# Attention scores of a decoder layer as float32r products over 64 rows of high and low parts, spread by transfers with 32 rows as outer dimension, and the maxima kept on the chip

## The chip, the cores and the metric

The kernel runs on one core of one Trainium2 chip. The metric is the device time of one execution in microseconds (us), as a median of several runs. PE is the engine for matrix products (PEld its weight loads), DVE, ACT and POOL work on vectors, and SP only issues transfers (DMA) here, all on one queue, in order. An engine works through its instructions in the order in which they were written to it.

## What is computed

For each of 32 batches of 256 tokens with 256 channels, the reference computes one decoder layer. All arrays are float32.

```
x = layernorm(x + ssm(x))                    # state-space mixer, 512 inner channels, 16 states
x = layernorm(x + attention(x, ctx, ctx))    # 16 heads of 16 channels, 256 keys
x = layernorm(x + experts(x))                # 8 experts, each with 32 tokens of every batch, 704 wide

scores = einsum('bhqd,bhkd->bhqk', q, k) / sqrt(16)
attn   = softmax(scores)                     # over the 256 keys
```

The mixer has a recurrence over the tokens, in chunks of 64, for each of 512 x 16 states. The change concerns the scores: `q` and `k` are 16 channels per head, and the softmax subtracts each query's largest score before the exponential.

## The kernel before, in words

**Stages.** The program holds no loop with waits of its own choice: a planner, run while the program is written, holds a clock for each engine, a cost for each kind of instruction (`MM`, `EV`, `VE`, `CV`, `GP`, L307 to L311) and some twenty chains of work (L1255 to L1276). `in_order` (L80) lets the chain whose next step can start first take its step, and so fixes the order of instructions on each engine for good. Semaphores then make each instruction wait for its data. The chains are the mixer (`pres`, `steps`, `decays`, `scan`, `weighted`, `sums`), the attention (`keys_ahead`, `keys`, `mixes`, `queries`, `maxima`, `attns`, `finishes`), the experts (`units`, `fetches` and others, in two sets of buffers), and `rest` (L364), which issues the transfers of weights that are needed later.

**The mixer.** Each batch takes 16 steps of 32 inner channels. A step loads `ld` by two transfers of 256 KB (L519), ACT makes the decays `da` (L573, four instructions), DVE makes the product `bu` (L602) and the recurrence `h` (L621), POOL multiplies `h` by `c_bc` (L637), and after every four steps PE sums the states into `y` (L651). There are 512 steps. There are six buffers for `h`, and three steps of `ld` are loaded ahead. Between these instructions the planner puts those of the other chains.

**The attention of a batch.**
- Keys are made some batches ahead (L691): PE `ps_qk`, ACT adds the bias into `k_flat` (two halves of 128 channels, L706), and a transfer stores it to `k_all` in DRAM (L710). The values take the same buffer afterwards. Queries do the same with `q_flat` and a DRAM tile `heads` (L801 to L806).
- `spread_heads` (L678) loads them back from DRAM so that a head's 16 channels lie at rows 0 to 15 (even heads) or 64 to 79 (odd heads) of `kT` and `qT`, eight heads (one half of the 16) with two transfers of 64 KB. The other rows of `qT` are zero; row 63 of each half of `kT` is one, all through the run (L271 to L277).
- `maxima` (L825) takes two heads at a time: `scores` (L809) issues four products of 63 rows (two heads on the two halves of PE's rows, two halves of the queries) into two PSUM banks; DVE takes the maximum over the keys (L838) into `tops`. After eight heads PE transposes `tops` (L844), ACT negates it into `rows` (L847), a transfer stores `rows` to DRAM (L852), and another loads them into row 63 of `qT` (L855).
- `attns` (L874) makes the scores again, keys against queries, over 64 rows: since row 63 of `kT` is one and that of `qT` the negated maximum, they come out lowered. ACT takes the exponential from PSUM (L894), PE multiplies by the values (L863), and `finish` (L924) divides, projects, normalizes and stores the batch to `x2d` (L969).

**The experts.** A unit is two blocks of 128 rows of four batches each (L978). For batches 24 to 31 a unit holds two experts for one group of four batches, so its last four units need batch 31 from `x2d`. A unit has products `ps_h` (L1133) and `ps_down` (L1212), and units are what the planner puts between the other work on PE. At most five PSUM banks (`RING`) serve everything but `bu` and `b_bc`.

The functions that the change touches, and their callers:

## Time and profile before

| | |
|---|---|
| runs | 2744.45, 2734.66, 2743.19 us; median 2743.19 |
| profiled execution | 2743.78 us, of which the span from the first to the last instruction is 2742.0 |
| busy, share of the span | PE 2466.3 us (90%), DVE 2380.6 (87%), ACT 2043.4 (75%), POOL 1643.7 (60%) |
| transfers | 505.86 MB in 491497 packets; the queue of SP fills 64.8% of 16 engines' span |
| mean granted PE clock | 0.959 |
| SP's waits on the maxima | 67.8 us for `rows` (ACT), 45.1 us for the store of `tops` |

How to read the rows. A line of groups has the source line, the engine, the operation, `output<-input`, the shapes and the count, then the busy time in us and the mean of one in ns, then the engine's idle time just before them and what ended most of it. A line of waits says who waited for whom: us in total, how often, the longest. The chain of work that ended last goes back from the last instruction, at each step to what released it; its rows are start and length in us. One product of float32 shows as two records of PE, and busy time counts overlapping records once. A row of stages has its bounds, its length, and the busy time and number of instructions of each engine.

The middle of the run is alike from some 140 us to 2500 us: the recurrence goes on, and the attention and experts of earlier batches run beside it. After the last recurrence the attention of the last batch is left, with the expert units that still wait, and after that batch's store four units.

### The profile page before, as it was taken

Reading aid. Unit: us, or ns where it says so; the run is one execution under the profiler, and the core shown is the slowest. Engines: PE = TensorE matmul, PEld = TensorE weight load, DVE = VectorE, ACT = ScalarE, POOL = GpSimd, SP = SyncE. Lnnn points to the kernel's source line nnn. Section 1 sums busy time; section 2 is a strip of 40 time slices with the busy share of each in tenths; the row PEclk is TensorE's granted clock in tenths of the full one; section 3 lists DMA queues with packets and bytes.
Section 4 is the critical chain, followed back from the end, with each engine's and each line's share of the span. In section 5 each row is a group of like instructions: output and inputs, shape, how many; then the busy total and the mean of one; then the engine's idle time right before and its main releaser. Section 6 shows DMA issues by size and latency. Waiting matters only on the chain.

```text
span 2742.0 us, 48659 instructions
## 1 busy us (share of the span) xinstructions
PE 2466.3 (90%) x16964; PEld 1705.3 (62%) x16964; DVE 2380.6 (87%) x2413; ACT 2043.4 (75%) x4327; POOL 1643.7 (60%) x1145
## 2 busy tenths in 40 slices
PE   5788989889899899989998989999999899998988
PEld 4565666566566666666666666665666566666767
DVE  4999999999999999999999999999999899896212
ACT  6887888888778878887878778888788788674331
POOL 4775766666666666575666665666666666553000
PEclk8899999999999999998999999999999999999999
DMA  7866666666676666676666666667666566666464
GB/s 203 228 199 176 193 187 181 189 191 191 187 199 186 181 167 190 176 197 177 167 198 187 198 175 186 187 177 195 190 197 179 163 172 180 185 174 181 150 195 144
DMA packets 491497, 505.86 MB, mean 184 GB/s; under 512 B 177204, under 2 KB 339252, under 8 KB 491252
## 3 DMA queue, kind: packets, MB, share of 16 engines
q1 hardware_dynamic: 491252, 502.75, 64.8%
q8 instruction: 135, 2.21, 0.4%
q14 instruction: 110, 0.90, 0.1%
HBM read 426.07 MB, written 76.55 MB: 183 GB/s over the span
## 4 chain that ended last, share of the span: by engine, by line
PE 29%; DVE 11%; ACT 8%; DMA 5%; issue 3%; POOL 1%; SPq 1%; DVEq 0%; ACTq 0%; POOLq 0%
PE ps_h L1133 8%; PE s L816 6%; DVE h L621 5%; PE ps_down L1212 4%; ACT da L573 3%; PE y L651 3%; DVE bu L602 2%; DVE tops L838 2%; PE ps_in L349 2%; PE ps_oT L863 2%; DMA ld<-dd 1%; DMA xe<-x2d 1%; PE ps_out L349 1%; PE ps_qk L349 1%; ACT es L894 1%
## 5 line engine op out<-in xcount | busy, mean ns | idle before, releaser
L637 POOL TENSOR_TENSOR h<-h,c_bc 128x1024 f32<-128x1024 f32 x512 | 1209.1, 2362 | 740.6 <-DVE h L621 627.0
L621 DVE TENSOR_TENSOR_SCAN h<-da,bu 128x1024 f32<-128x1024 f32 x512 | 1168.9, 2283 | 50.4 <-ACT da L573 5.8
L573 ACT ACTIVATE da<-ld,a_neg 128x252 f32<-128x252 f32 x2048 | 864.6, 504 | 188.3 <-DVE h L621 138.4
L602 DVE TENSOR_TENSOR bu<-ld,b_bc 128x1024 f32<-128x1024 f32 x512 | 626.1, 1223 | 19.9 <-DMA ld<-dd 8.0
L816 PE MATMUL s<-kT,qT 63*128 63x256 f32 x2048 | 345.4, 416 | 45.6 <-DVE tops L838 22.8
L894 ACT ACTIVATE es<-s 128x512 f32<-128x512 f32 x512 | 277.9, 594 | 140.6 <-PE s L816 75.9
L838 DVE TENSOR_REDUCE tops<-s 128x2 f32<-128x512 f32 x512 | 325.2, 677 | 41.6 <-PE s L816 41.1
L1133 PE MATMUL ps_h<-x2T,w 128*128 128x256 f32 (+2 forms) x1536 | 343.5, 368 | 9.5 <-ACT es L894 1.7
L816 PE MATMUL s<-qT,kT 64*128 64x256 f32 x2048 | 313.8, 405 | 22.5 <-DMA qT<-tops 13.0
L651 PE MATMUL y<-h,sel_y 128*32 128x256 f32 x4096 | 280.8, 397 | 52.3 <-POOL h L637 36.9
L816 PEld LDWEIGHTS s<-kT,qT 63*128 63x128 f32 x2048 | 213.8, 193 | 151.9 <-DVE tops L838 50.8
L1133 PEld LDWEIGHTS ps_h<-x2T,w 128*128 128x128 f32 (+1 forms) x1536 | 246.7, 186 | 89.7 <-issue 35.1
L349 PE MATMUL ps_in<-xT,w_in 128*128 128x256 f32 x1024 | 258.4, 397 | 8.7 <-ACT da L573 2.6
L816 PEld LDWEIGHTS s<-qT,kT 64*128 64x128 f32 x2048 | 200.9, 189 | 102.3 <-issue 39.6
L651 PEld LDWEIGHTS y<-h,sel_y 128*32 128x32 f32 x4096 | 131.8, 113 | 177.4 <-POOL h L637 55.1
L349 PEld LDWEIGHTS ps_in<-xT,w_in 128*128 128x128 f32 x1024 | 192.8, 196 | 60.4 <-issue 12.9
L420 POOL TENSOR_TENSOR u<-u,shifted 128x512 f32<-128x512 f32 x128 | 151.4, 1183 | 39.7 <-ACT u L407 34.7
L323 POOL TENSOR_SCALAR ln_rstd<-ln_mv 128x2 f32<-128x2 f32 x96 | 20.9, 218 | 254.2 <-DVE ln_mv L320 250.0
L407 ACT ACTIVATE shifted<-ps_in,tap_b,conv_w 128x256 f32<-128x256 f32 x256 | 130.8, 567 | 22.5 <-PE ps_in L349 10.9
L863 PE MATMUL ps_oT<-es,v 128*32 128x256 f32 x2048 | 142.4, 391 | 3.7 <-DVE h L1197 1.2
L349 PE MATMUL ps_out<-w_out,yg 128*128 128x256 f32 x512 | 117.6, 383 | 0.4 <-DVE yg L667 0.4
L375 ACT ACT_TABLE_LOAD x90 | 115.5, 1283 | 1.4
(135 smaller groups left out, 2987.5 us busy)
## 6 DMA issues: line engine op xcount, KB each, us to landing
ld<-dd SPq DMA_DIRECT2D x1024, 256.0 KB
w<-in_w SPq DMA_DIRECT2D x128, 352.0 KB
x<-in_x SPq DMA_DIRECT2D x64, 256.0 KB
dd<-delta SPq DMA_DIRECT2D x32, 512.0 KB
dd<-u SPq DMA_DIRECT2D x32, 512.0 KB
w<-in_w SPq DMA_DIRECT2D x32, 384.0 KB
w13y<-in_w SPq DMA_DIRECT2D x32, 352.0 KB
c_bc<-bcd SPq DMA_DIRECT2D x64, 128.0 KB
```

What stands on the lines that cost most here:

```text
L349: nc.tensor.matmul(ps[:, j, :], l, r, start=(k == 0), stop=(k == len(terms) - 1))
L420: nc.gpsimd.tensor_tensor(u[:, cc], u[:, cc], at, ALU.add)
L573: nc.scalar.activation(da[:, g, q].rearrange("p (k t) -> p k t", t=CHUNK)[:, :, 1:], loads[i][:, 0, g].rearrange("p (k t) -> p k t", t=CHU ...
L602: nc.vector.tensor_tensor(bu, loads[i][:, 1].unsqueeze(2).to_broadcast([P, GB, NQ, L]), b_bc.unsqueeze(1).to_broadcast([P, GB, NQ, L]), AL ...
L621: nc.vector.tensor_tensor_scan(h.rearrange("p g q t -> p (g q t)"), das_of.pop(i).rearrange("p g q t -> p (g q t)"), bu.rearrange("p g q t ...
L637: nc.gpsimd.tensor_tensor(hs[i], hs[i], c_bc, ALU.mult)
L651: nc.tensor.matmul(y[32 * j : 32 * j + 32, :], sel_y[:, g, :], hs[i - NJ + 1 + j][:, g, q, :], start=(g == 0 and q == 0), stop=(g == GB - ...
L816: nc.tensor.matmul(s[:, t, :], left[r : r + n, g, t * P : (t + 1) * P], right[r : r + n, g, :], start=True, stop=True,)
L838: nc.vector.tensor_reduce(top[:, h % 2, h // 2, :], s, AX.X, ALU.max)
L863: nc.tensor.matmul(oT[32 * j : 32 * j + 32, :], v[:, k, 4 * g + j, :], ess[j][:, k, :], start=(k == 0), stop=(k == 1), tile_position=(0, 3 ...
L894: nc.scalar.activation(es, s, AF.Exp, scale=1.0 / DK**0.5)
L1133: nc.tensor.matmul(ps[:m, i, :], w_tiles[u, which, e][k][:, f * P : f * P + m], right, start=(k == 0), stop=(k == 1),)
```

## The change

The scores are made from two parts of each number. POOL copies `k_flat` (`q_flat`) to a float32r tile `hi`, which rounds it, and takes `lo` = full - `hi` in place (new `parts_of`). Both parts go to DRAM, and they come back so that each head has 64 rows, which hold, for each of the 16 channels, the four combinations of a part of `q` with a part of `k`. So one float32r product over 64 rows gives the score. To get these rows, the query's transfer reads 32 rows (part, channel) and writes each twice, 256 KB a transfer with runs of 4 KB; the key's transfers read 32 rows (channel, part) and write them once each, 128 KB, two for the two copies. Weights' columns and the biases are reordered so that the channel is the outer index; POOL does it for `w_k` and `w_q` at the start (`ordered`), and all but one of the late transfers go out before it.

The maxima don't go to DRAM. POOL copies `tops` to `padded` in high and low parts, PE transposes it twice (128 rows each), and ACT writes the negated maxima as `mT`. In `attns` a second product adds them to the scores in PSUM: weights `pick`, which has ones at the two rows (high and low) of the head, on all 128 columns, times `mT`. So `maxima` has the same number of products as before, and `attns` twice as many. Row 63 of `kT` and `qT` and their fills are gone. The planner's costs are changed in places (`MM`, `EV`, `VE`, `CV`, `GP`, and those of layer norm, decays and scan), which moves instructions of all chains.

The diff, cut to what the text speaks of:

```diff
@@ -115,7 +116,7 @@
 
     x2d = dram.tile([B, L, D], F32, name="x2d")
 
-    k_all = dram.tile([B, D, L], F32, name="k_all")
+    k_all = dram.tile([B, DK, 2, 2 * NG, 2, L], F32, name="k_all")
     v_all = dram.tile([B, L, D], F32, name="v_all")
 
     ph = ctx
@@ -163,18 +164,31 @@
         dma(t, a[name].partition_broadcast(P))
         return t
 
-    def heads(n):
+    def heads(n, tag):
 
         w = wp.tile([P, 2, D], F32, tag="w_" + n, name="w_" + n)
+        raw = unit1.tile([P, 2, D], F32, tag=tag, name="raw_" + n)
         src = a["w_" + n].rearrange("(k p) (h c) -> p k h c", p=P, c=32)
         for k in range(2):
-            dst = w[:, k].rearrange("p (h c) -> p h c", c=DK)
+            dst = raw[:, k].rearrange("p (h c) -> p h c", c=DK)
             dma(dst, src[:, k, :, :DK])
         bias = wp.tile([P, 2], F32, name="b_" + n)
-        for g in range(NG):
-            r = 64 * (g % 2)
-            src = a["b_" + n].rearrange("(j c) g -> j c g", c=32)[:, :DK, g : g + 1]
-            dma(bias[r : r + 64, g // 2 : g // 2 + 1], src)
+        src = a["b_" + n].rearrange("(g1 j c) (i g2) -> j g2 g1 c i", g1=2, j=2, c=32, g2=2)
+        for j in range(2):
+            for g in range(NG):
+                dma(bias[NG * j + g :: 2 * NG, :], src[j, g // 2, g % 2, :DK])
+
+        def ordered():
+            for k in range(2):
+                for i in range(2):
+                    at = slice(i * P, (i + 1) * P)
+                    nc.gpsimd.tensor_copy(
+                        w[:, k, at].rearrange("p (c j g) -> p g j c", j=2, c=DK),
+                        raw[:, k, at].rearrange("p (g j c) -> p g j c", j=2, c=DK),
+                    )
+            spend("POOL", 1.6)
+
+        orders.append(ordered)
         return w, bias
 
 
@@ -206,13 +220,13 @@
             dma(at, src[j, g].unsqueeze(1).to_broadcast([DL, NL, NDC * NS]))
     nc.scalar.preload_act_table_set("natural_log_exp_and_others")
 
-    later = []
+    later, orders = [], []
     now, dma = dma, lambda dst, src: later.append((dst, src))
-    w_k, b_k = heads("k")
+    w_k, b_k = heads("k", "att")
     w_v = weight("w_v", D, D)
     b_out = row("b_out")
     w_out = weight("w_out", DI, D)
-    w_q, b_q = heads("q")
+    w_q, b_q = heads("q", "oT")
     w_o = weight("w_o", D, D)
     b_o = row("b_o")
     b_v = wp.tile([P, 2, 1], F32, name="b_v")
@@ -268,13 +282,22 @@
     nc.gpsimd.memset(v[:, :, :, DK : DK + 1], 1.0)
 
 
-    kT = keep.tile([P, HG, L], F32, name="kT")
-    last = small.tile([P, 1], F32, tag="ln_st", name="last")
-    at = ident.rearrange("p (j c) -> p j c", c=HR)[:, :, HR - 1]
-    nc.vector.tensor_reduce(last, at, AX.X, ALU.add)
-    nc.vector.tensor_copy(kT.rearrange("p g t -> p (g t)"), last.to_broadcast([P, HG * L]))
-    qT = keep.tile([P, HG, L], F32, name="qT")
-    nc.gpsimd.memset(qT, 0.0)
+    kT = keep.tile([P, HG, L], F32R, name="kT")
+    qT = keep.tile([P, HG, L], F32R, name="qT")
+    mTs = [keep.tile([P, L], F32R, name=f"mT_{i}") for i in range(2)]
+    padded = keep.tile([P, 2, 2, HR], F32R, name="padded")
+    nc.gpsimd.memset(padded.bitcast(F32), 0.0)
+    pick = keep.tile([P, HG], F32R, name="pick")
+    picked = small.tile([P, HG], F32, tag="ln_st", name="picked")
+    nc.vector.tensor_reduce(
+        picked.rearrange("p (i g) -> p i g", i=2),
+        ident.rearrange("p (j r) -> p j r", r=HR)[:, :, : 4 * NG].rearrange(
+            "p j (i s g) -> p i g j s", i=2, s=2
+        ),
+        AX.XY,
+        ALU.add,
+    )
+    nc.vector.tensor_copy(pick, picked)
 
     tops = [keep.tile([P, 2, 4, 2], F32, name=f"tops_{i}") for i in range(2)]
 
@@ -304,11 +327,11 @@
         return ps_mm.tile([P, 2 * L], F32, tag="mm", name=name)
 
 
-    MM = 0.47
-    EV = {1: 0.47, 2: 0.6, 4: 1.06}
-    VE = {1: 0.41, 2: 0.69, 4: 1.23}
-    CV = 0.565
-    GP = {1: 0.7, 2: 1.27, 4: 2.36}
+    MM = 0.49
+    EV = {1: 0.42, 2: 0.56, 4: 1.05}
+    VE = {1: 0.41, 2: 0.66, 4: 1.225}
+    CV = 0.535
+    GP = {1: 0.7, 2: 1.23, 4: 2.36}
 
     def layernorm(tiles, t):
 
@@ -330,7 +353,7 @@
             nc.scalar.activation(
                 x, x, AF.Identity, bias=off[:, i, :], scale=rstd[:, i, :]
             )
-        return spend("ACT", 0.6 * n)
+        return spend("ACT", 0.55 * n)
 
     def transposes(src):
 
@@ -363,9 +386,13 @@
 
     def rest():
 
-        while later:
+        while len(later) > 1:
             yield 0.0, "SP"
             dma(*later.pop(0))
+        yield clock.at["SP"] + 2 * LANDING, "POOL"
+        while orders:
+            orders.pop(0)()
+        dma(*later.pop(0))
 
     xps, dds, sress, bcds, ygs, us, spread, silus = {}, {}, {}, {}, {}, {}, {}, []
     gated, stored = {}, []
@@ -576,7 +603,7 @@
                         AF.Exp,
                         scale=a_neg[:, j, g, c * NQ + q : c * NQ + q + 1],
                     )
-            decayed[i] = spend("ACT", GB * NQ * 0.5)
+            decayed[i] = spend("ACT", GB * NQ * 0.43)
 
     read = {-1: 0.0}
 
@@ -626,7 +653,7 @@
                 op0=ALU.mult,
                 op1=ALU.add,
             )
-            recurred[i] = spend("DVE", 2.29)
+            recurred[i] = spend("DVE", 2.285)
             read[i] = max(multiplied, decayed[i])
 
     def weighted():
@@ -675,6 +702,23 @@
     kts, qts, tts, vts, x1Ts, attended, oSs, ending = {}, {}, {}, {}, {}, [], [], []
     scored = {}
 
+    def parts_of(n, b, full, t, d):
+
+        hi = unit1.tile([P, 2, L], F32R, tag="hi", name=f"{n}_hi_{b}")
+        lo = full.bitcast(F32R)
+        yield t, "POOL"
+        nc.gpsimd.tensor_copy(hi, full)
+        nc.gpsimd.tensor_tensor(lo, full, hi.bitcast(F32), ALU.subtract)
+        t = spend("POOL", 2 * GP[2])
+        yield t, "SP"
+        for s, part in enumerate((hi, lo)):
+            part = part.bitcast(F32)
+            if n == "q":
+                dma(d[:, s].rearrange("i c x t -> (c x) i t"), part)
+            else:
+                at = d[:, s].rearrange("c x i t -> c x (i t)")
+                dma(at, part.rearrange("p i t -> p (i t)"))
+
     def spread_heads(b, dst, d, t, there):
 
         yield t, "SP"
@@ -682,8 +726,16 @@
             if b:
                 yield lambda: max(t, scored[b - 1, half]) if (b - 1, half) in scored else None, "SP"
             for j in range(2):
-                src = d.rearrange("(i g j c) t -> i j c g t", i=2, j=2, c=DK)[half, j]
-                dma(dst[HR * j : HR * j + DK, 4 * half : 4 * half + 4, :], src)
+                at = dst[HR * j : HR * (j + 1), NG * half : NG * (half + 1), :].bitcast(F32)
+                if dst is qT:
+                    src = d[half, :, :, NG * j : NG * (j + 1)]
+                    src = src.rearrange("s c g t -> (s c) (g t)").unsqueeze(1)
+                    at = at.rearrange("p g t -> p (g t)")
+                    dma(at, src.to_broadcast([2 * DK, 2, NG * L]))
+                else:
+                    src = d[:, :, NG * j : NG * (j + 1), half].rearrange("c s g t -> (c s) g t")
+                    for s in range(2):
+                        dma(at[2 * DK * s : 2 * DK * (s + 1)], src)
             there[b, half] = clock.at["SP"] + LANDING
 
     made = []
@@ -706,8 +758,7 @@
             flat = unit1.tile([P, 2, L], F32, tag="k_flat", name=f"k_flat_{b}")
             tk = biased(flat, AF.Identity, b_k, ps, 0)
             done(1, tk)
-            yield tk, "SP"
-            dma(k_all[b].rearrange("(m p) t -> p m t", p=P), flat)
+            yield from parts_of("k", b, flat, tk, k_all[b])
             yield from take(1, rank, t0)
             ps, t = product(
                 "ps_v",
@@ -801,13 +852,11 @@
             flat = unit1.tile([P, 2, L], F32, tag="q_flat", name=f"q_flat_{b}")
             tq = biased(flat, AF.Identity, b_q, ps, 0)
             done(1, tq)
-            yield tq, "SP"
-            d = bcd.tile([D, L], F32, tag="heads", name="heads")
-            dma(d.rearrange("(m p) t -> p m t", p=P), flat)
+            d = bcd.tile([2, 2, DK, 2 * NG, L], F32, tag="heads", name="heads")
+            yield from parts_of("q", b, flat, tq, d)
             yield from spread_heads(b, qT, d, clock.at["SP"] + LANDING, qts)
 
-    def scores(heads, left, right, n):
-
+    def scores(heads, left, right, lowered):
 
         ss = [bank("s").rearrange("p (t n) -> p t n", t=2) for _ in heads]
         for t in range(2):
@@ -815,12 +864,22 @@
                 g, r = h // 2, HR * (h % 2)
                 nc.tensor.matmul(
                     s[:, t, :],
-                    left[r : r + n, g, t * P : (t + 1) * P],
-                    right[r : r + n, g, :],
+                    left[r : r + HR, g, t * P : (t + 1) * P],
+                    right[r : r + HR, g, :],
                     start=True,
-                    stop=True,
+                    stop=not lowered,
                 )
-        return ss, spend("PE", 2 * MM + 0.2)
+            for h, s in zip(heads, ss):
+                g, r = h // 2, HR * (h % 2)
+                if lowered:
+                    nc.tensor.matmul(
+                        s[:, t, :],
+                        pick[r : r + HR, g : g + 1].to_broadcast([HR, P]),
+                        mTs[g // NG][r : r + HR, :],
+                        start=False,
+                        stop=True,
+                    )
+        return ss, spend("PE", 0.7 if lowered else 0.4)
 
     def maxima():
 
@@ -832,28 +891,30 @@
             h = 0
             while h < 8:
                 yield from take(2, 2, t0)
-                ss, ts = scores(range(8 * half + h, 8 * half + h + 2), qT, kT, HR - 1)
+                ss, ts = scores(range(8 * half + h, 8 * half + h + 2), qT, kT, False)
                 for s in ss:
                     yield ts, "DVE"
                     nc.vector.tensor_reduce(top[:, h % 2, h // 2, :], s, AX.X, ALU.max)
                     t = spend("DVE", VE[2])
                     done(1, t)
                     h += 1
+            yield t, "POOL"
+            r = 2 * NG * half
+            hi, lo = padded[:, :, :, r : r + NG], padded[:, :, :, r + NG : r + 2 * NG]
+            full = top.rearrange("p j g t -> p t j g")
+            nc.gpsimd.tensor_copy(hi, full)
+            nc.gpsimd.tensor_tensor(lo, full, hi.bitcast(F32), ALU.subtract)
+            t = spend("POOL", 0.5)
             yield from take(1, 1, t)
-            ps = bank("ps_m")[:H, :P]
-            nc.tensor.transpose(ps, top.rearrange("p j g t -> p (j g t)"), ident)
-            yield spend("PE", 0.2), "ACT"
-            rows = unit2.tile([H, P], F32, tag="rows", name="rows")
-            nc.scalar.activation(rows, ps, AF.Identity, scale=-1.0)
-            t = spend("ACT", 0.35)
+            ps = bank("ps_m")[:, :L]
+            for k in range(2):
+                src = padded[:, k].rearrange("p j r -> p (j r)").bitcast(F32)
+                nc.tensor.transpose(ps[:, k * P : (k + 1) * P], src, ident)
+            yield spend("PE", 0.6), "ACT"
+            nc.scalar.activation(mTs[half], ps, AF.Identity, scale=-1.0)
+            t = spend("ACT", EV[1])
             done(1, t)
-            yield t, "SP"
-            d = bcd.tile([2, 4 * L], F32, tag="tops", name="tops")
-            dma(d.rearrange("j (i n) -> (j i) n", n=P), rows)
-            yield clock.at["SP"] + LANDING, "SP"
-            dst = qT[HR - 1 :: HR, 4 * half : 4 * half + 4]
-            dma(dst.rearrange("j g t -> j (g t)"), d)
-            tts[b, half] = clock.at["SP"] + LANDING
+            tts[b, half] = t
 
     def attend(g, ess):
 
@@ -883,7 +944,7 @@
                 while g < 2 and len(ess) < 4:
                     yield from take(2, 2, tq)
                     h = 8 * half + 4 * g + len(ess)
-                    ss, ts = scores(range(h, h + 2), kT, qT, HR)
+                    ss, ts = scores(range(h, h + 2), kT, qT, True)
                     if g and not ess:
                         yield lambda: vts.get(b), "PE"
                         yield from take(1, 3, max(te, vts[b]))
```

More of the change, by code (lines that the diff above doesn't have):

```diff
@@ L9 @@
 F32 = mybir.dt.float32
+F32R = mybir.dt.float32r
 AF = mybir.ActivationFunctionType
```

## The prediction

> **What bounds the kernel now.** I read the stages first, because one average would mix three different limits. The stretches are the start up to the steady state, the scan (its last start is at 2511.1 us), the last batch's attention up to the store of its result at 2635.9, and the end. Columns: bounds, length, busy time (instructions) of PE, PEld, DVE, ACT and POOL, granted clock, DMA share, GB/s.
>
> ```profile
> 0.00:137.00 137.00, 94.97 (x443) 68.00 (x444) 93.65 (x71) 101.22 (x203) 84.64 (x69) 0.81 0.80 215
> 137.00:2511.00 2374.00, 2170.99 (x15115) 1475.30 (x15114) 2231.83 (x2223) 1871.14 (x3992) 1539.13 (x1027) 0.97 0.66 184
> 2511.00:2636.00 125.00, 115.72 (x883) 90.52 (x882) 35.77 (x74) 53.74 (x100) 11.84 (x27) 0.96 0.54 170
> 2636.00:2742.00 106.00, 84.68 (x528) 71.52 (x526) 19.36 (x46) 17.30 (x33) 8.07 (x24) 0.91 0.53 169
> ```
>
> From 137 to 2511 DVE is busy 94%, PE 91%. What ends DVE's idle time there says how much of PE's load matters (the waits of DVE in this stretch):
>
> ```profile
> DVE tops L838 <- PE s L816: 22.5, 26, 3.5
> DVE yg L667 <- PE y L651: 15.9, 13, 3.0
> DVE xe L1224 <- PE ps_down L1212: 13.0, 4, 6.9
> DVE x L964 <- PE ps_o L349: 10.2, 9, 2.6
> ```
>
> All named waits of that list add up to 84 us, 78 of them on PE. DVE's idle time is 2374 - 2232 = 142; the other 58 us are gaps of some 0.1 us at each scan and product, which no change of PE touches. So DVE bounds this stage, and a PE that cost nothing could win at most 78 us of it.
>
> After 2511 it is otherwise. DVE is busy 29%, PE 93%: the last batch must pass ps_out, layer norm, queries, heads through DRAM, maxima, attention and the store, then four expert units follow. In the chain of work that ended last, in this stretch, I read two things: PE works on expert units between the steps of that batch, and the maxima's trip through DRAM stands on the path.
>
> ```profile
> 2522.13 3.46 PE ps_out L349 x16
> ...
> 2528.07 8.26 DMA tops<-rows
> 2536.43 4.64 DMA qT<-tops
> 2541.11 2.08 PE s L816 x8
> ...
> 2617.87 5.68 PE ps_h L1133 x48
> ...
> 2635.91 3.21 DMA x2d<-x
> ```
>
> **The change part by part.**
>
> *Scores on PE.* The groups of instructions give what they cost:
>
> ```profile
> L816 PE MATMUL s<-kT,qT 63*128 63x256 f32 x2048 | 345.4, 416 | 45.6 <-DVE tops L838 22.8 <-DMA qT<-heads 5.9 <-ACT u L407 2.8
> L816 PE MATMUL s<-qT,kT 64*128 64x256 f32 x2048 | 313.8, 405 | 22.5 <-DMA qT<-tops 13.0 <-DVE tops L838 2.7 <-DVE yg L667 2.2
> L637 POOL TENSOR_TENSOR h<-h,c_bc 128x1024 f32<-128x1024 f32 x512 | 1209.1, 2362 | 740.6 <-DVE h L621 627.0
> ```
>
> The code issues 1024 products for each of the two, so a float32 product is two records. Two heads on the two row halves form a pair: 1024 pairs cost 659.2 us, 0.64 each; close together a call of two pairs takes 1.06 (8 records in the chain), 0.53 a pair. Afterwards there are 512 pairs for the maxima, 512 for attention, and 512 more that subtract the maxima: 1536. No float32r product is in this trace. Lower bound: the densest records of the trace, y's, 32 in 1.86 us, 0.06 each, 0.12 for two. Upper bound: the same 0.53. Nearest row: 48 ps_h records of 128 columns, each with a 128-column weight load of its own as every score has, take 5.68 us, 0.118 each; two per pair give 0.12 (side by side) to 0.24 (one after the other). I take 0.20. With the trace's spread of 0.64/0.53 = 1.21 that is 1536 x 0.20 x 1.21 = 372 us, a saving of 287. The maxima's transpose becomes two of 128 rows: 64 x some 0.25 = 16 more. PE falls from 2466 to about 2195. PE breaks even at 659/1536 = 0.43 a pair.
>
> Against the change speaks a rule of the Trainium skill, "TensorE: Matmul & The Clock Gate" (LDWEIGHTS): a weight load takes time by its columns, P/1.2 ns, so 107 ns for 128, however few the rows are. An estimate by that page: the loads would set 0.21 a pair and the sum would be 390 us, where the row's 0.12 would make it 223; the 0.118 above, measured with a load in each, leaves room for either.
>
> *The clock.* The granted clock was 0.81 from 68 to 137 us, where PE was busy 54.7 of 69 us, against 0.97 in the scan stage. A PE that is relieved may be granted less. If all of the scan stage's PE work (2171 - 0.95 x 271 + 32 for two more units, 1945) went at 0.90 instead of 0.97, it would be 2097 of some 2340, still under DVE's 94%. The gain would shrink, not vanish.
>
> *POOL.* Each batch's keys and queries get a copy and a subtraction of 128x512. Bounds: half of a 0.95 us memset of 128x1024, and 1.27 (x<-x,b_out, 128x512). At 1.27: 2.54 x 64 = 163 us, and 128 small ones for the maxima at some 0.2 to 0.7 (the layer norm's, L323 and L324), about 50. In the scan stage POOL goes from 65% to some 74%. The cover: the scan can run on while POOL is late, six h buffers against groups of four; of DVE's waits only 1.0 us is on POOL L637 now. If that cover goes, each 2.54 reaches DVE (a rival below).
>
> *DMA.* Per batch, keys and queries go out twice (256 to 512 KB each) and come back as 1024 KB instead of 256 each, and the maxima's four small ones go: about 1056 to 3072 KB, 65 MB in all. q1 moved 502.75 MB in 64.8% of 16 engines' span; at that rate 65 MB are 8.4 points more, about 73% in the scan stage. ld transfers, which feed DVE, share the queue; DVE waited 8.0 us for them in the whole run (L602, "DMA ld<-dd 8.0"). I price it at 0 to 25 us, take 6. On SP, issues rise from 2300 to 2372, mostly kT's (128 to 256) and k_all/heads (64 more), less 128 for the maxima; at 0.42 us an issue (median for kT, qT) 30 us of SP time, against 113 us of SP waits on the maxima (67.8 on rows, 45.1 on tops) that go. SP now also waits for POOL's parts, with ld transfers behind it in order: its cost is in the 6.
>
> *Start.* 8 more bias transfers (8 x 0.42 = 3.4) and 8 small reorderings on POOL, ahead of the second batch's u; a DVE fill of 2.9 us goes, which DVE had time for (it waited 2.9 for a_all after it). +2.
>
> *The order.* Of the instructions each kernel writes out, 704 PE products came after the last y; now 563. Products of ps_h there fall from 376 to 280: two expert units (48 each) move ahead of the last scan, with 2 x 4 us on DVE (h products, xe sum, layer norm; x2 tops more), and 24 attention products less. Attention of batch 30 is through when the scan ends.
>
> **The sum.** *Scan stage:* of the 78 us of PE waits, those for scores (22.5) should all but go, -20, and I halve the other 55, since PE goes from 91% to 83%, -28; two units more on DVE, +9; DMA, POOL and SP, +6. That is -33. *Last batch:* from last y (2517.5) to the store took 118 us. Rebuilt from its rows: ps_out done after 8 (as now); norm and transposes to 15; query product after one ps_h group, 18; on ACT a silu with two table loads first, q_flat at 23; POOL's split 2.5, two issues, landing 3, spread 1.7, landing 3: first maxima at 36 (now 41). Then 8 tops of 0.65 with unit products between, 8; pad, transpose and copy 3; second half's maxima run beside the first half's 8 exps (0.54 each); second half's maxima, exps, two oT, and the rows from there to the store, together 26 more: 73. So -45, since about 30 us of unit products, a 13 us round trip by DRAM and scores at 1.06 a call are gone. The last 106 us keep their four units: 0.
>
> 2743.8 (the profiled execution; span 2742.0, so 1.8 around it; the median of the runs is 2743.2) + 2 - 33 - 45 = **2668 us**, 2.8% less.
>
> **The rivals.**
> 1. *PE's waits nearly vanish.* 78 us less 9 for units and 9 new, with the same end and a quicker chain (-55): 2743.8 - 60 - 55 = 2629. For it: DVE had 95.6% from 137 to 300, where attention had not begun in earnest. Against it: order is fixed, and POOL and ACT remain.
> 2. *New waits take the old ones' place.* The scan stage keeps its 2374 (halved PE waits given back to POOL parts, DMA, clock); only the end gains, 30 to 45: 2701 to 2716. For it: 0.94 on DVE leaves little; DMA at 73%.
> 3. *POOL's split reaches the scan (slower).* One hi buffer serves keys and queries, POOL is in order, and its copy waits till the earlier part has left; h products queue behind, then y, then h buffers. Price: 163 us if every split comes through, against 76 won; it decides from 47% of the split time on. At all of it: 2668 + 163 = 2831. Against it: the 1.0 us above.
> 4. *float32r is no quicker per product.* 1536 x 0.64 = 989, +330 of PE busy; the scan stage's PE work, 2171 + 313 + 47, is 2531; at 91% filling 2781: +407, about 3150. It decides from 0.43 a pair.
>
> **How the numbers follow.** Forecast (2648 to 2692): 0.50. Rival 1: 0.13. Rival 2: 0.21, of which 0.02 fall within 0.5% of no change. Between that and no gain: 0.05 within 0.5%. Rival 3: 0.06, rival 4: 0.05, both slower. Within 0.5% (13.7 us, about what a measurement of this kernel can tell from no change): 0.07; faster 0.82; slower 0.11. The range 2618 to 2724 takes in the first three cases, leaves 0.18 out, and covers bounds of the pair price (0.12 to 0.24) and of DMA; the pair price of 0.53 is rival 4.
>
> **What would show it.** Score records of about 0.2 us a pair and PE near 2200; DVE's total within 5 us of 2380.6 with its waits on PE halved; last scan near 2480 (2511 now); store of the last batch some 73 us after the last y, and 106 from there on. Wrong would be: waits of DVE h or bu on POOL or ld over 40 us; a granted clock below 0.9 in the scan stage; score records as long as now.

## The result, and the profile after

The kernel with the change is **slower**: 2847.94 us as a median of 4 runs (2846.36 to 2851.55), beside 2743.82 for the kernel before on the same chip (4 runs). By the medians that is 104 us more; the ratio is 1.0389, 95% interval 1.0367 to 1.0411. The forecast of 2668 and its range (2618 to 2724) both missed.

The stages of the kernel after, cut at the same events as before (last start of the recurrence at 2649.6 us, store of the last batch at 2742.1), with the columns of the table of stages shown with the prediction:

```profile
0.00:137.00 137.00, 88.18 (x418) 63.07 (x422) 82.69 (x65) 100.94 (x201) 87.05 (x83) 0.81 0.79 213
137.00:2650.00 2513.00, 2135.81 (x14542) 1472.38 (x14536) 2255.38 (x2252) 1910.81 (x4036) 1680.42 (x1279) 0.90 0.75 203
2650.00:2742.00 92.00, 77.12 (x556) 59.21 (x550) 29.05 (x62) 35.01 (x67) 14.71 (x33) 0.92 0.64 189
2742.00:2844.00 102.00, 77.31 (x496) 66.41 (x496) 15.65 (x36) 15.32 (x30) 5.39 (x16) 0.87 0.42 137
```

The loss lies in the second row alone. It is 139 us longer, although PE is busy 35 us less in it and DVE does nearly the same work (2255 us, 24 more, for units that moved ahead and work that came over from the first stretch). DVE's share fell from 94% to 90%: it waits for more. PE's granted clock fell from 0.97 to 0.90, and the DMA share rose from 0.66 to 0.75. The last two rows are 37 us shorter together, in the direction of the forecast.

What DVE waits for in that stage (the first rows of its waits, 137 to 2650 us: total, how often, longest):

```profile
DVE tops L897 <- PE s L865: 103.2, 61, 8.5
DVE yg L694 <- PE y L678: 34.0, 22, 4.1
DVE rec L1001 <- PE ps_oB L996: 13.0, 7, 4.6
```

The wait of the maxima for their scores was 22.5 us, which the prediction had as all but gone; it is 103.2. All DVE waits on PE add up to 194.5 us in this stage; before they were 78. These 116 us and the 24 of DVE's own work make up the 139. So the next question is what PE waits for (its waits, whole run):

```profile
PE s L865 <- DMA qT<-heads: 64.4, 38, 5.4
PE s L865 <- DVE tops L897: 61.7, 105, 2.7
...
PE ps_in L372 <- ACT xT L412: 28.5, 10, 3.5
PE ps_m L912 <- POOL padded L906: 26.1, 17, 6.7
```

The first row was 5.9 us before: the queries' transfers arrive after PE has reached the scores, and PE, in order, stands still with everything behind it. The same happens on ACT for the mixer's loads, where 44.4 us (first row, the kernel before) have become 128.2 (the kernel after):

```profile
ACT da L573 <- DMA ld<-dd: 44.4, 17, 6.0
ACT da L600 <- DMA ld<-dd: 128.2, 55, 9.6
ACT da L600 <- DVE h L648: 113.9, 95, 3.2
```

The groups of scores, to be set against the two L816 rows of before:

```profile
L865 PE MATMUL s<-qT,kT 64*128 64x256 f32 x1024 | 198.4, 346 | 39.9 <-DVE tops L897 15.2 <-ACT es L955 12.7 <-DVE yg L694 6.9
L865 PE MATMUL s<-kT,qT 64*128 64x256 f32 x1024 | 187.7, 379 | 145.1 <-DMA qT<-heads 64.4 <-DVE tops L897 46.5 <-ACT da L600 10.7
L875 PE MATMUL s<-mT,pick 64*128 64x256 f32 x1024 | 167.6, 310 | 0.0
```

A float32r product is one record, where float32 had two. The three groups cost 553.7 us in place of 659.2, a saving of 105 us.

Landing times below are worked out from the trace's landing events, from the start of an issue to its last landing, as means over a run. A query transfer took 3.38 us before and takes 6.42; a key transfer 3.69 and 4.12; `ld` 4.24 and 4.90. The planner reckons with 3.5 (`LANDING`).

### The profile page after: what moved, and what is told of

Its sections match the earlier page's. It is cut to its first block, busy times and chain, and to the rows that moved or that the text cites. A ratio compares the mean times of both kernels' runs of the same rounds, so it can differ in the third digit from the quotient of the medians.

```text
span 2844.6 us, 47193 instructions
## 1 busy us (share of the span) xinstructions
PE 2378.4 (84%) x16004; PEld 1661.1 (58%) x16004; DVE 2382.8 (84%) x2413; ACT 2062.1 (72%) x4331; POOL 1787.6 (63%) x1409
## 3 DMA queue, kind: packets, MB, share of 16 engines
q1 hardware_dynamic: 525012, 568.82, 73.6%
## 5 line engine op out<-in xcount | busy, mean ns | idle before, releaser
L600 ACT ACTIVATE da<-ld,a_neg 128x252 f32<-128x252 f32 x2048 | 863.9, 502 | 264.9 <-DMA ld<-dd 128.2
L897 DVE TENSOR_REDUCE tops<-s 128x2 f32<-128x512 f32 x512 | 323.7, 679 | 116.6 <-PE s L865 116.1
L1194 PE MATMUL ps_h<-x2T,w 128*128 128x256 f32 (+3 forms) x1632 | 390.5, 387 | 19.2 <-DMA w<-in_w 6.1
L1194 PEld LDWEIGHTS ps_h<-x2T,w 128*128 128x128 f32 (+1 forms) x1632 | 279.5, 201 | 99.6 <-issue 29.7
L372 PE MATMUL ps_in<-xT,w_in 128*128 128x256 f32 x1024 | 290.1, 434 | 36.8 <-ACT xT L412 28.5
L865 PE MATMUL s<-kT,qT 64*128 64x256 f32 x1024 | 187.7, 379 | 145.1 <-DMA qT<-heads 64.4
L372 PEld LDWEIGHTS ps_in<-xT,w_in 128*128 128x128 f32 x1024 | 212.4, 216 | 91.1 <-ACT xT L412 34.0
L865 PEld LDWEIGHTS s<-kT,qT 64*128 64x128 f32 x1024 | 117.0, 221 | 238.1 <-issue 86.1
L865 PE MATMUL s<-qT,kT 64*128 64x256 f32 x1024 | 198.4, 346 | 39.9 <-DVE tops L897 15.2
L865 PEld LDWEIGHTS s<-qT,kT 64*128 64x128 f32 x1024 | 129.0, 206 | 114.1 <-issue 31.0
L875 PE MATMUL s<-mT,pick 64*128 64x256 f32 x1024 | 167.6, 310 | 0.0
L875 PEld LDWEIGHTS s<-mT,pick 64*128 64x128 f32 x1024 | 125.6, 210 | 0.2
```

What stands on the lines that cost most here:

```text
L372: nc.tensor.matmul(ps[:, j, :], l, r, start=(k == 0), stop=(k == len(terms) - 1))
L600: nc.scalar.activation(da[:, g, q].rearrange("p (k t) -> p k t", t=CHUNK)[:, :, 1:], loads[i][:, 0, g].rearrange("p (k t) -> p k t", t=CHU ...
L865: nc.tensor.matmul(s[:, t, :], left[r : r + HR, g, t * P : (t + 1) * P], right[r : r + HR, g, :], start=True, stop=not lowered,)
L875: nc.tensor.matmul(s[:, t, :], pick[r : r + HR, g : g + 1].to_broadcast([HR, P]), mTs[g // NG][r : r + HR, :], start=False, stop=True,)
L897: nc.vector.tensor_reduce(top[:, h % 2, h // 2, :], s, AX.X, ALU.max)
L1194: nc.tensor.matmul(ps[:m, i, :], w_tiles[u, which, e][k][:, f * P : f * P + m], right, start=(k == 0), stop=(k == 1),)
```

## The experiments

Four theories were to be told apart. **A**: the bytes of the spread. Either (A1) the queries' transfers, on the path from projection to maxima, land late, and PE holds up DVE; or (A2) all bytes count alike, through the full queue and `ld`. **B**: the planner's changed costs. **C**: the lower clock of PE. **D**: POOL's split.

### The planner's costs alone, both ways

```diff
 # e1: the kernel before, with the figures of after (e2: the reverse; it keeps its 0.4 and 0.7 for the scores)
-    MM = 0.47
+    MM = 0.49
...
-            decayed[i] = spend("ACT", GB * NQ * 0.5)
+            decayed[i] = spend("ACT", GB * NQ * 0.43)
```

> The kernel before with nothing but the changed planner costs (MM, EV, VE, CV, GP, layer norm, decays, scan). Theory A (the spread's bytes: queries land late, PE waits in order, DVE behind it) expects no loss from the costs: 2744, at most 0.5% off. Theory B (the plan: costs below the measured times, 0.43 for a decay that takes 0.50, make an order that is too tight) expects a good part of the 104 us: 2780 to 2840.

> The changed kernel with the planner costs of before put back (its own 0.4 and 0.7 for the scores kept). Theory A expects 2835 to 2855, no change. Theory B expects 2750 to 2790, the loss mostly gone.

Measured: the kernel before with the new figures 2743.81, ratio 0.9976 (0.9955 to 0.9997); the kernel after with the old ones 2889.72, ratio 1.0507 (1.0468 to 1.0547). The new figures lose nothing by themselves, and the change without them is worse by about 1.2% of the time, which no theory had expected. B falls as the cause of the loss. The second run also says that the plan alone can move this kernel by over 1%.

### The spread's bytes

```diff
 # e3: one head of four arrives (the rest of kT and qT stays zero); e5: queries only; e6: keys only
-                    dma(at, src.to_broadcast([2 * DK, 2, NG * L]))
+                    dma(at[:, :L], src[:, :, :L].to_broadcast([2 * DK, 2, L]))
...
-                        dma(at[2 * DK * s : 2 * DK * (s + 1)], src)
+                        dma(at[2 * DK * s : 2 * DK * (s + 1), :1], src[:, :1])
```

> The changed kernel, with each of the transfers that spread kT and qT cut to one head of its four: the same number of transfers and the same order, a quarter of their bytes (as before the change). Three quarters of the heads keep the zeros of a fill at the start, so their scores are not computed from data. Theory A expects the queries to land 3 us earlier and 2740 to 2790. Theory B, and theory C (PE is granted a lower clock, 0.90 for 0.97, because it is less busy, and everything on PE is slower), expect 2830 to 2850.

> The changed kernel, with only the transfers of qT cut to one head of four (the other heads of qT keep zeros, so their scores are not the right ones); kT's are whole. Theory A1 (the queries land late on the path from the projection to the maxima, and PE waits for them in order) expects most of the 78 us of the run that cut both: 2775 to 2800. Theory A2 (all bytes count alike, since they delay ld and everything else on the queue) expects half: 2805 to 2820.

> The changed kernel, with only the transfers of kT cut to one head of four (the other heads of kT keep zeros); qT's are whole. The keys are made batches ahead. Theory A1 expects little: 2830 to 2850. Theory A2 expects half: 2805 to 2820.

In the run with both cut, the spread brings as many bytes as before the change, in the transfers of the kernel after. Measured: both cut, 2770.07, ratio 1.0071 (1.0046 to 1.0095); queries alone, 2792.59, ratio 1.0174 (1.0154 to 1.0194); keys alone, 2834.78, ratio 1.0342 (1.0318 to 1.0366). By the distance of these ratios from 1.0389, three quarters of the spread's bytes cost 3.2% or some 87 us (78 by the medians themselves, taken on two chips), the queries' 2.2% or 59, the keys' 0.5% or 13 (the two single cuts leave some 15 us that come only with both). Keys and queries were cut by the same number of bytes, yet the queries bring over four times as much. Landing fits this: cut queries land in 4.00 us in place of 6.42, and with only the keys cut the queries still take 6.43. Two rows of PE's waits with the queries cut, and one of DVE's:

```profile
PE s L866 <- DVE tops L898: 65.8, 99, 3.0
...
PE s L866 <- DMA qT<-heads: 29.7, 13, 4.7
```

```profile
DVE tops L898 <- PE s L866: 61.0, 47, 9.9
```

PE's wait for queries falls from 64.4 to 29.7 us and DVE's for scores from 116.1 to 61.0 (both whole run). This is A1. What speaks against A2, the way through `ld`, is that both cuts relieve `ld` alike: it lands in 4.56 us with the queries cut and in 4.65 with the keys cut (4.90 in the kernel after), and ACT's wait for it, 128.2 us in the kernel after, falls even further with the keys cut (first row: queries cut; second: keys cut):

```profile
ACT da L601 <- DMA ld<-dd: 98.3, 48, 5.3
ACT da L601 <- DMA ld<-dd: 86.3, 42, 7.7
```

That relief came with 13 us in the second run, so A2 is the small part. The run with both cut also has a landing of 4.40 for `ld` and half the wait for it:

```profile
L602 ACT ACTIVATE da<-ld,a_neg 128x252 f32<-128x252 f32 x2048 | 863.0, 502 | 204.7 <-DVE h L650 136.5 <-DMA ld<-dd 60.5 <-DVE tops L899 4.5
```

### The planner told that the spread lands late

```diff
-            there[b, half] = clock.at["SP"] + LANDING
+            there[b, half] = clock.at["SP"] + 2 * LANDING
```

> The changed kernel, with the planner told that the spread lands 7.0 us after its issue, not 3.5 (the trace shows 6.4 on average for qT). Nothing but the order changes. Theory A expects PE's wait for qT (58 us) to go from the scan stage and 2780 to 2820; if the bytes delay ld as well, the rest stays. Theories B (costs of ACT, DVE) and C expect 2835 to 2855.

Measured: 2825.67, ratio 1.0275 (1.0237 to 1.0314). PE's wait for queries falls to 19.3 us, but only about 31 us of the time come back, a little less than theory A had expected:

```profile
DVE tops L897 <- PE s L865: 85.6, 60, 6.9
DVE yg L694 <- PE y L678: 45.3, 28, 5.8
```

A plan with the right landing removes a part of the wait, not the bytes' whole price: over the whole run these rows were 116.1 and 44.4 in the kernel after, and with the queries' bytes gone (the runs above) they are at 61.0 to 63.9 and 34.5 to 37.3. PE's wait for queries is shorter here (19.3) than with the queries cut (29.7), and yet the time is 1.0% longer. So either PE's standing still is not all that the late queries cost, or the later plan costs something itself; no run separates the two.

I then also gave the planner longer scores, since I took a call of four records of some 0.35 us to need more than 0.4 us:

```diff
-        return ss, spend("PE", 0.7 if lowered else 0.4)
+        return ss, spend("PE", 2 * MM + (0.7 if lowered else 0.2))
```

> The kernel after, with two of the planner's figures made longer: the spread's transfers land at 7.0 us instead of 3.5, as in the earlier run, and a call of four score products is costed as before the change (2 MM + 0.2 = 1.18 us, 1.68 with the maxima) instead of 0.4 and 0.7. Four records of about 0.35 us make some 1.4 us, so the planner's 0.4 puts the reduces and exponentials too early in DVE's and ACT's orders. Theory A with the plan's share: DVE's wait of tops on scores falls from 103 us to under 60, and the time to 2770 to 2805 (the run with late landing alone had 2826). Rival, the waits are those of transfers and a slower clock whatever the order: 2815 to 2850.

Measured: 2906.44, ratio 1.0591 (1.0558 to 1.0624): a miss, and worse. DVE's wait for scores did fall below 60, and the last recurrence starts at 2560.4 instead of 2649.6; but from there to the end it is now 348 us, not 195:

```profile
DVE xe L1285 <- PE ps_down L1273: 127.0, 18, 18.6
DVE tops L897 <- PE s L865: 55.9, 37, 7.0
```

The planner's costs decide how many expert units fit beside the recurrence. Costs that are too long on PE push units behind its end (`ps_h` has 1104 records after the last `y` in this run, 560 in the kernel after), where PE alone works on them. So a stage's gain has to be read together with what it leaves for later.

### The maxima on the chip alone

```diff
 # the kernel before, float32 scores over the 16 channels (other rows zero), no parts; maxima as in the kernel after
+                    nc.tensor.matmul(
+                        s[:, t, :],
+                        pick[r : r + HR, g : g + 1].to_broadcast([HR, P]),
+                        mTs[g // NG][r : r + HR, :],
+                        start=False, stop=True,
+                    )
...
-        return ss, spend("PE", 2 * MM + 0.2)
+        return ss, spend("PE", 2 * MM + (0.5 if lowered else 0.2))
```

> The kernel before with one part of the change: maxima split by POOL, transposed, and subtracted by a second float32r product. The scores stay float32 over the 16 channels, and keys and queries are stored and spread as before. Theory A (the bytes of the spread are the loss) expects 2700 to 2745, since the maxima's trip through DRAM goes and no bytes come. A theory that the second product and the small POOL steps are the loss expects 2780 to 2840.

Measured: 2802.47, ratio 1.0212 (1.0192 to 1.0232), where theory A had expected 2700 to 2745: a miss. PE is busy 2538.1 us (before 2466.3). The last recurrence starts early, at 2489.4, with 75 us of waits on PE in its stage; the loss is behind it, 305 us to the end in place of 231, with 957 PE products after the last `y` (before 704). So the removal of the DRAM trip gave no net gain here. I read this as the added products taking room from the units; part of it can be the plan, which has 1.44 us for a call of scores with maxima here and 0.7 in the kernel after. No run separates the two.

### Score products issued twice in the kernel after

```diff
+                for again in range(2):
                     nc.tensor.matmul(s[:, t, :], left[...], right[...],
-                        start=True, stop=not lowered)
+                        start=True, stop=not lowered or not again)
```

> The changed kernel with each of its 2048 score products issued twice (the second overwrites the first), in an order that is the same otherwise: 1024 pairs more, some 120 us of PE at its full clock. Theory C (PE is granted less because it is idle more, and that is what costs) expects the granted clock to rise from 0.89 towards 0.93 and the time to stay at 2840 to 2860 or fall. If PE's load still ends on the path, 2880 to 2950 with the clock as it is. Theory A has 2850 to 2900, as PE waits for transfers part of the time anyway.

Measured: 2868.55, ratio 1.0452 (1.0410 to 1.0494), about 17 us more than the kernel after, for 1024 more pairs (some 118 us at 0.115; PE's busy time rose by 63). The clock rose from 0.893 to 0.918, and the time rose beyond the 2840 to 2860 that theory C had. Most of the added work costs no time: PE's amount of work is not the main thing that sets the time here.

### POOL's split

```diff
-        nc.gpsimd.tensor_copy(hi, full)
-        nc.gpsimd.tensor_tensor(lo, full, hi.bitcast(F32), ALU.subtract)
         t = spend("POOL", 2 * GP[2])
...
-        for s, part in enumerate((hi, lo)):
+        for s, part in enumerate((lo, lo)):
```

> The kernel after without the POOL copy and subtraction of keys and queries; both transfers of parts read the unrounded tile (so high and low parts are left out and scores are wrong), and the planner spends the same, so every order stays. About 120 us of POOL work go, and 3.75 us from the way from a query product to its spread. Theory A (bytes): 2835 to 2855, the queue moves the same bytes. Theory D (the split delays queries and POOL's other products): 2800 to 2830, with PE's wait for qT down by over 20 us.

> The run with a quarter of the spread's bytes (2770), and in addition no POOL split (as in the run beside it; three heads of four hold no data and the parts are left out). Theory A: what is left above the kernel before is the four parts' second transfers and the planner's short scores, 2755 to 2775. Theory D: the split is the rest, 2725 to 2750.

Here both stored parts are the unrounded tile. Measured: 2852.73, ratio 1.0403 (1.0363 to 1.0442), and with the quarter spread 2777.30, ratio 1.0127 (1.0095 to 1.0158), just above theory A's range. Neither is faster than its counterpart with the split (1.0389 and 1.0071). POOL loses 116 us of work, and PE's wait for queries stays (75.6 us). D falls.

### float32r alone, in the kernel before

```diff
-    kT = keep.tile([P, HG, L], F32, name="kT")
+    kT = keep.tile([P, HG, L], F32R, name="kT")
...
-    qT = keep.tile([P, HG, L], F32, name="qT")
+    qT = keep.tile([P, HG, L], F32R, name="qT")
```

> The kernel before with its key and query tiles declared float32r, written by the same transfers from the same bytes: the two score products are one record instead of two, nothing else moves, maxima still go out and come back. The low bits of keys, queries and maxima are left out. It is the change's saving on PE alone. If the prediction's working of the scan stage holds (PE's waits halve), 2675 to 2710. If PE's saving is worth little by itself, since DVE at 94% is the bound and the transfers of maxima stay: 2715 to 2745. PE's busy time should fall by 150 to 290 us.

Measured: 2758.47 (10 runs), ratio 1.0045 (1.0027 to 1.0062). This is the change's saving on PE without its bytes, split and second product, in the same order of instructions, **and it gains nothing**; it is above both ranges that I had given it. The scan stage of that run:

```profile
137.00:2511.00 2374.00, 1996.11 (x13045) 1329.38 (x13043) 2210.56 (x2200) 1857.92 (x3970) 1529.91 (x1022) 0.90 0.65 183
```

The groups of the states' sums (`y`; first row, the kernel before) and of scores:

```profile
L651 PE MATMUL y<-h,sel_y 128*32 128x256 f32 x4096 | 280.8, 397 | 52.3 <-POOL h L637 36.9 <-ACT es L894 7.6 <-ACT k_flat L355 3.7
L652 PE MATMUL y<-h,sel_y 128*32 128x256 f32 x4096 | 311.9, 424 | 82.8 <-POOL h L638 37.2 <-ACT es L895 12.4 <-DVE tops L839 6.9
...
L817 PE MATMUL s<-kT,qT 63*128 63x256 f32 x1024 | 180.4, 370 | 94.4 <-DVE tops L839 63.1 <-DMA qT<-heads 9.3 <-ACT es L895 4.7
...
L817 PE MATMUL s<-qT,kT 64*128 64x256 f32 x1024 | 152.7, 344 | 47.9 <-DMA qT<-tops 13.0 <-DVE tops L839 10.4 <-DVE x L773 4.1
```

The scores cost 333.1 us, 326 less than before. But PE's total fell by only 168 (2466.3 to 2298.8): the clock went from 0.97 to 0.90 in this stage, and other products grew (`y` from 397 to 424 ns, `ps_h` from 395 to 423). DVE's waits on PE in its scan stage rose from 78.0 to 97.8 us, and the last recurrence starts at 2533.7, 22.6 later. The first rows of these waits:

```profile
DVE yg L668 <- PE y L652: 24.2, 21, 3.5
DVE x L965 <- PE ps_o L350: 20.7, 9, 5.6
DVE tops L839 <- PE s L817: 16.2, 19, 4.5
```

The maxima do wait less for their scores, 16.2 in place of 22.5, but the waits for other products grew by more (`yg` was 15.9, `x` 10.2).

The clock of the whole run is 0.898, as low as in the kernel after (0.893), and the loss is 0.45%. So a lower clock by itself does not make the 3.9%: C falls as the main cause.

The trace's clock is 1.0 or 0.5, in stretches of 3.41 us or multiples of that. In the scan stage it is 0.5 for 143 us before, and for 474 us in this run. DVE's gaps of over 0.3 us, laid over these stretches (worked out from the trace's records), come to:

| kernel | us at clock 0.5 | DVE's gaps there | share of that time | share of the time at 1.0 |
|---|---|---|---|---|
| before | 143 | 17 | 12% | 2.8% |
| before, float32r scores | 474 | 45 | 9% | 3.0% |
| the same, scores twice | 362 | 43 | 12% | 2.9% |
| quarter spread | 425 | 53 | 12% | 3.4% |
| after | 516 | 97 | 19% | 4.8% |

With float32r scores the gaps at full clock take the same share as before: the shorter scores removed next to nothing there. What is new, 28 us, lies in the stretches at half clock.

Three more runs ask whether the clock takes the saving back, or the order was not made for it.

```diff
 # e13: the run above, each score product issued twice
+                for again in range(2):
...
 # e14 and e15: the run above, the planner's score call shortened
-        return ss, spend("PE", 2 * MM + 0.2)
+        return ss, spend("PE", 0.4)    # e15: 0.8
```

> The kernel before with float32r scores, each product issued twice into the same place (the second one the same as the first): 2,048 pairs more at 0.115 us, some 235 us of PE work at full speed of the 300 that float32r saved. The clock should go up from 0.90 to about 0.93 to 0.95. Theory clock (the lower clock is what takes the saving back): other products shorten to their lengths before, the time falls to 2735 to 2750 or below. Theory order (PE was no bound; what it holds up is set by when a call's inputs are there): 2755 to 2780, as twice the scores in the kernel after gave 20 us more.

> The kernel before with float32r scores, and the planner told that a score call takes 0.4 us on PE instead of 1.18. If the saving comes only where the order moves units into the freed time, as the prediction had it: 2690 to 2735, with fewer products left behind the last scan than the kernel before has. If four records of 0.35 us make the plan too short, DVE's wait of tops on scores grows from 32 us to over 60 and the scan stage is longer: 2755 to 2800.

> As the run beside it with 0.8 us a score call, between the kernel's 1.18 and 0.4. The prediction's saving: 2700 to 2735. No bound on PE: 2745 to 2775.

Measured: scores twice, 2756.36, ratio 1.0055 (1.0040 to 1.0070); planned at 0.4, 2767.03, ratio 1.0097 (1.0079 to 1.0116); at 0.8, 2755.03, ratio 1.0056 (1.0041 to 1.0071). The stage row with scores issued twice:

```profile
137.00:2511.00 2374.00, 2067.96 (x14996) 1442.41 (x14997) 2213.95 (x2203) 1861.86 (x3976) 1532.68 (x1022) 0.92 0.64 183
```

72 us more work on PE in this stretch, and the time is the same, with DVE's waits on PE at 94.5 us in its scan stage: PE's amount of work does not bound the kernel before either. That run gave back 0.02 of 0.07 of the clock, too little to say what a full return would bring. The shorter plans move units ahead of the end, as the prediction wanted (from last recurrence to end 199.9 us at 0.4, 230.9 before), but the recurrence ends 56 us later: what the tail gains the scan stage gives back, and more. That the maxima would then wait over 60 us, as I had expected, did not come (39.3 in the whole run, 31.9 with the longer plan).

## Why the prediction was wrong, point by point

The pieces of the profiled spans: first recurrence 43.9 to 48.1 us (+4), first to last recurrence 2467.2 to 2601.5 (+134), last recurrence to end 230.9 to 195.0 (-36). The forecast was +2, -33, -45. So it is the scan stage that the prediction had wrong, by 167 us, and two of its steps made most of that.

- **"I halve the other 55, since PE goes from 91% to 83%"** is, with the -20 for the scores before it, the step whose mechanism failed. It took waits on PE as a part of PE's load. With float32r alone PE's busy time falls by 168 us and the waits rise by 20, where -48 was forecast; with scores issued twice they stay. I read them as the waits of single calls, which come when their inputs or banks do; the runs show only that they do not follow PE's amount of work. The saving is worth less than nothing here (a loss of 0.3 to 0.7% by the intervals of these two runs).
- **"DMA, POOL and SP, +6"**, of which DMA was "0 to 25 us": three quarters of the bytes cost some 78 to 87 us. The share of the queue was forecast well (73%; measured 0.75 in the stage, 73.6% in all). What I left out is that a query transfer of 256 KB lands in 6.42 us, not 3, on a path where PE waits in order. This is the larger term: with a quarter of the spread the last recurrence starts at 2573.9, 75.7 us sooner than in the kernel after. Roughly, 68 us for the waits and 70 for the bytes (75.7 less the 6) are 138 of the 167; the rest stays open.
- **Price of a pair.** 553.7 us over 1536 pairs is 0.36, not 0.24. The dense price was at the lower bound, as the timeline of a call shows at full clock (start, length):

```profile
1309.18 0.39 PE L865 MATMUL s<-qT,kT 64*128 64x256 f32 x2
1309.40 0.28 PE L875 MATMUL s<-mT,pick 64*128 64x256 f32 x2
1309.52 0.28 PE L865 MATMUL s<-qT,kT 64*128 64x256 f32 x2
1309.63 0.28 PE L875 MATMUL s<-mT,pick 64*128 64x256 f32 x2
```

  Later pairs start 0.11 to 0.12 us apart, but every call of two to four pairs pays the length of a record as well, and a fifth of the stage runs at half clock. I compared whole calls of 1.06 us with a dense row. By the rule I weighed from the Trainium skill, "TensorE: Matmul & The Clock Gate" (LDWEIGHTS), my estimate with one load after the other was 0.21. The measured 0.115 a pair leaves no room for that and is near the row's 0.12.
- **The clock.** I wrote that the gain at 0.90 "would shrink, not vanish". The clock came out at 0.90, and the gain vanished. A busy total below DVE's share was the wrong test: in the runs of the kernel before and of float32r alone, in the half-clock stretches DVE's gaps take 9 to 12% of the time, at full clock 3%, and the mean clock does not show that difference.
- **The order.** 563 products after the last `y` in place of 704 do shorten the tail. I priced the two units moved at 9 us on DVE. With the score call planned at 0.4 us alone (the kernel before, float32r), the scan stage grows by 56 and the tail falls by 31.
- **"PE near 2200", "DVE's total within 5".** PE came to 2378.4, since the pairs were dearer and the clock lower; DVE to 2382.8, 2.2 above its 2380.6, as forecast. With DVE's work unchanged, all of the loss is waiting. The prediction's signs of being wrong did not point to it: they looked for waits of `h` or `bu` on POOL or `ld` over 40 us, which are 0.5 and 8.9, while the loss came to DVE through PE. The clock stood at its mark of 0.9.
- **The tail.** From last `y` (2655.9) to the store it takes 86 us; the forecast was 73, before 118. The chain of that stretch shows the largest missing piece, a landing of 8.22 us where I took 3:

```profile
2687.59 8.22 DMA qT<-heads
2695.95 0.59 PE s L865 x2
...
2717.22 2.38 DVE tops L897 x4
...
2734.03 3.24 PE ps_o L372 x8
...
2742.11 2.14 DMA x2d<-x
```

  The maxima's trip is gone as foreseen. The end from there is 102.5 us (forecast 106).
- **The rivals.** The slower side came, by neither of the mechanisms I had named for it. POOL's split (rival 3) did not reach the scan: DVE waited 0.5 us for it, a split takes 1.88 us and not 2.54 (copy 0.61, subtraction 1.27), and taking it away gains nothing. float32r was quicker per product (rival 4). Rival 2, new waits in place of the old ones, was right in kind and far too small.

Put together, by the ratios to the kernel before on each run's own chip: float32r alone +0.45%; with the score call planned at 0.4 us +0.97%; the whole change with a quarter of the spread +0.71%; all of it +3.89%. So the spread's added bytes carry some four fifths of the loss, and a loss as large as the rest is there already with float32r and a shorter plan. That the on-chip maxima and the second transfers add nothing beyond that in the kernel after is only inferred from these figures; in the kernel before, with float32 scores, the on-chip maxima alone cost 2.1%.

What stays open: whether the half-clock stretches cause DVE's added gaps in the float32r run or follow from PE's idle time around them. Both fit the table; no run held the clock up with the saving kept. It also stays open whether the late queries cost more than PE's wait for them shows, and where the 15 us come from that only both cuts together bring.

## What to carry to other kernels

Before an engine's saving is counted, ask which waits of the bounding engine end on its amount of work and which on a single call's inputs; doubling a part of that engine's work in a run is a cheap test, and here it moved the time by nothing in the kernel before and by 17 us in the kernel after. Bytes that stand on a path between two engines are priced by their landing time at the queue's new load, not by the queue's share. Where a planner fixes the order, read the stage and the tail together, since its costs move work from one to the other.

## What the runs showed of the hardware

- The granted clock took two values, 1.0 and 0.5, in stretches that are multiples of 3.41 us; less PE work gave more half-clock stretches (6% of the scan stage before, 20% with float32r scores, 15% with those issued twice).
- A float32r product of 64 rows by 256 columns is one record and a pair on the two row halves follows the last by 0.11 to 0.12 us at full clock (timeline at 1309 us); a float32 call of two pairs took 1.06 us, 8 records.
- A transfer of 64 KB of queries landed in 3.38 us and one of 256 KB in 6.42, with the queue at 0.66 and 0.75; keys of 128 KB in 4.12.
- On POOL a rounding copy of 128x512 to float32r took 0.61 us and the subtraction 1.27.
